# One product of a two-level Strassen scheme moved from a plain blocked product to an inner seven, with its operand sums kept in DRAM

## The chip, the cores and the metric

The kernel runs on one core of a Trainium2 chip. The time is the device time of one execution in microseconds (us); the kernel before has a median of 562.96 us over 3 runs (562.48 to 563.15). Lower is better. The engines are called as in the profile: PE (matrix products), DVE (vector), ACT (scalar), POOL (GpSimd), and SP, which here only issues DMAs. ACT and POOL issue DMAs too.

## The reference

Two layers on 16 graphs of 1024 nodes and 64 channels, with one 1024 x 1024 matrix `adj`:

```
# layer 0
Q, K, V = x Wq' + bq, x Wk' + bk, x Wv'
s = softmax(Q K', over the queries) ;  x = layernorm(x + (s adj) V)
# layer 1, both supports are adj
x1 = adj x ;  x2 = 2 adj x1 - x ;  x = layernorm(x + [x, x1, x2, x1, x2] weight + bias)
```

All is float32. Layer 1 can be written with two products by `adj`: with the five blocks W0..W4 of `weight`, z = x (W1 + W3) + adj (2 x (W2 + W4)), and the layer is x + x (W0 - W2 - W4) + bias + adj z. The change lies in the second product, adj z.

## The kernel before, in words

`xs` holds x with the nodes on the partitions (8 blocks of 128 nodes, index k) and 8 pairs of graphs (index p, 2 x 64 channels each). So adj z is a product of 1024 x 1024 by 1024 x 1024. It is done in Winograd's form of Strassen's scheme: seven products of 512 x 512 blocks, numbered 1 to 7. The left operand of product n is `SIDE[n]` (a block of adj or a sum of blocks, on chip), the right one is `B_F[n]` (a block of z or a sum). Most of these products are cut once more in the same way ("an inner seven"): class `Inner` (L931) forms four sums of quarters of the left operand (`of_a`), four of the right (`of_b`), and `Inner.step` (L953) runs one of seven 256 x 256 x 512-column pieces: four matmuls of 256 columns (`product`, L863) and then one to three additions of the result to its places (`step`, L872). The order is `STEPS`; `CHAIN = {6: 1, 3: 5, 4: 7}` says that the pieces 6, 3 and 4 add onto the PSUM bank of 1, 5 and 7. Such a piece can start only when the bank's earlier contents have been read out. `TO` says to which quarters a piece is added: 9 additions of 128x512 for seven pieces.

The work around the change, in program order (the order is written by hand; each engine runs its own instructions in that order, and an instruction that waits holds all behind it on its engine):

- Before adj z, the product for z itself is done. Its products 3 and 4 are inner sevens (`z3`, `z4`, L1104 to L1109). The sums of `SIDE[3]` for z3 are made by POOL into the two tiles `V` (`own(1)`), which product 5 of adj z overwrites later.
- adj z runs its products 1, 2, 5, 6 and 7 as inner sevens. While product 6 runs, POOL makes the left sums of product 7. Product 7 (L1177) is written to `W`, which takes the place of `SIDE[1]`. While product 7 runs, `added` (L987, its DMAs are L991 in the profile) issues six DMAs from POOL that add the tiles V and U to `xs` on their way (512 KB each, `accum_op=ADD`): V to rows k 4 to 7 and V to rows k 0 to 3 of the pairs 4 to 7, then U to rows k 4 to 7 of the pairs 0 to 3 (L1202).
- Then `wide_step` (L1185) does product 3 plainly: for each of four row blocks four matmuls of 512 columns over k, and one addition of 128x512 into `xs` (L1194). Product 4 follows in the same way, with its last row blocks cut narrower (L1220 to L1223).
- `add_w` (L1053) adds W to `xs` on DVE: twice to pairs 4 to 7, and twice (L1213, L1216) to pairs 0 to 3, rows k 4 to 7, which are the rows that product 4 writes.
- The last layernorm is done in pieces (`Norm`, L996) as rows come complete: `square` on ACT, `variance` (a DVE reduction, a DVE addition, and a power of -1/2 on POOL, L494), `out` (the scaling, and the DMA of the result). With `fast` the scaling of two row blocks is two DVE instructions, without it sixteen ACT instructions of 128x64 each. The four pieces of pairs 4 to 7 are `late[0]` to `late[3]` (rows 4-5, 6-7, 0-1, 2-3), the seven pieces of product 4 are `norms`.

Of the kernel before, what the change touches and what calls it, by code (L numbers as in the profile page):

```python
# [9 lines left out]
FP = mybir.dt.float32  # L10
AF = mybir.ActivationFunctionType
ALU = mybir.AluOpType
# [14 lines left out]
def gnn_kernel(  # L27
# [13 lines left out]
    nc = tc.nc  # L41
    N, B, C = out.shape
    P = 128
    K8 = N // P
    NP = B // 2
    HP = NP // 2
    H = 512
# [14 lines left out]
    dram = ctx.enter_context(tc.tile_pool(name="dram", bufs=2, space=bass.MemoryType.DRAM))  # L62
# [21 lines left out]
    xs = big.tile([P, NP, K8, P], FP, tag="xs", name="xs")  # L84
# [86 lines left out]
    K4 = K8 // 2  # L171
    Q = H // 2
    S = big.tile([P, 3, K4, H], FP, tag="s", name="S")

    def a_block(r, c):

        return aT[:, K4 * c : K4 * (c + 1), H * r : H * (r + 1)]

    SIDE = {
        1: a_block(0, 0), 2: a_block(0, 1), 3: S[:, 2], 4: a_block(1, 1),  # L180
        5: S[:, 0], 6: S[:, 1], 7: a_block(1, 0),
    }
# [12 lines left out]
    def quarter(big_tile, h, r, c):  # L195

        t = big_tile[:, K4 * r : K4 * (r + 1), h * H + c * Q : h * H + (c + 1) * Q]
        return t.rearrange("p k (q f) -> p q k f", q=2)
# [361 lines left out]
    t = [quarter(XB, 0, r, c) for r, c in ((0, 1), (0, 0), (1, 0), (1, 1))]  # L560
    hop_0 = Hop(lambda r, c: x_quarter(0, r, c), into(UY, 0), t, u, FIRST)
    t = [quarter(XB, 1, r, c) for r in range(2) for c in range(2)]
# [156 lines left out]
    def whole_run():  # L719
        hop, n, group = runs.pop(0)  # L720
        po = f_tile(f"p{n}")
        hop.product(po, n, group, True)
        return lambda: hop.evict(po, n, group)

    late = [whole_run() for _ in range(2)]
    tail, before = None, None
    for p in range(NP):
        q = p - 1
        for m in range(K8):
# [17 lines left out]
            late = []  # L747
# [105 lines left out]
    q = NP - 1  # L853
    for_pool, for_vector = [], []

    def behind(pool=2, vector=1):

        for _ in range(min(vector, len(for_vector))):
            for_vector.pop(0)()
        for _ in range(min(pool, len(for_pool))):  # L860
            for_pool.pop(0)()
# [24 lines left out]
    t = [quarter(UY, 0, r, c) for r in range(2) for c in range(2)]  # L886
# [13 lines left out]
    def z_block(r, c):  # L900
        return XB[:, K4 * r : K4 * (r + 1), ts(c, H)]

    T_F = [UY[:, K4 * r : K4 * (r + 1), ts(c, H)] for r in range(2) for c in range(2)]
    B_F = {
        1: z_block(0, 0), 2: z_block(1, 0), 3: z_block(1, 1),
        5: T_F[0], 6: T_F[1], 7: T_F[2], 4: T_F[3],
    }
# [10 lines left out]
    def tiles(*tags):  # L918
        return [
            att.tile([P, N], FP, tag=tag, name=f"in_{tag}", bufs={"e": 4, "xT": 2, "GT": 2}.get(tag, 1))  # L920
            for tag in tags
        ]

    def blocks_of(t, n):

        return [
            t_[:, ts(j, 2 * n)].rearrange("p (k f) -> p k f", k=2)
            for t_ in t for j in range(N // (2 * n))
        ]
# [28 lines left out]
    def of_full(n, tags):  # L958

        t = tiles(*tags)  # L960
        return Inner(
            n, lambda r, c: B_F[n][:, 2 * r : 2 * r + 2, ts(c, Q)],
            blocks_of(t[:2], Q), blocks_of(t[2:], Q),
        )

    def of_z(n, sa, tb):

        return Inner(n, lambda r, c: hop_z.side[n][:, c, 2 * r : 2 * r + 2], sa, tb)
# [7 lines left out]
    def own(c):  # L976

        t = [att.tile([P, 2, K4, P], FP, tag="e", name=f"own{c}", bufs=4) for c in range(2)]
        return t, lambda r, c: t[c][:, :, 2 * r : 2 * r + 2].rearrange("p q g f -> p g q f")

    def in_x(r, c):
        def d(r_, c_):
            p, k = HP * c + 2 * c_, K4 * r + 2 * r_
            return xs[:, p : p + 2, k : k + 2].rearrange("p q g f -> p g q f")
        return d

    def added(t, r, c):  # L987

        def do(j):
            p = HP * c + 2 * j  # L990
            nc.gpsimd.dma_start(xs[:, p : p + 2, K4 * r : K4 * (r + 1)], t[j], accum_op=ALU.add)  # L991
        return [lambda j=j: do(j) for j in range(2)]
# [55 lines left out]
    W = SIDE[1].rearrange("p k (q f) -> p k q f", f=P)  # L1048
# [4 lines left out]
    def add_w(c, i):  # L1053

        x_ = xs[:, HP * c : HP * (c + 1), K4 + i : K4 + i + 2]
        w_ = W[:, i : i + 2].rearrange("p k q f -> p q k f")
        nc.vector.tensor_tensor(x_, w_, x_, ALU.add)
# [33 lines left out]
    U, d_u = own(0)  # L1091
# [5 lines left out]
    for kk, banks in (0, None), (2, (w[1], w[0])):  # L1097
# [4 lines left out]
    V, d_v = own(1)  # L1102
    t = [v.rearrange("p q k f -> p (q k f)") for v in V]
    z3 = of_z(  # L1104
        3, blocks_of(t, Q),
        [SIDE[1][:, k, 0:Q].rearrange("p (k f) -> p k f", k=2) for k in range(K4)],
    )
    t = tiles(*X[:3])
    z4 = of_z(4, blocks_of(t[:2], Q), blocks_of(t[2:], P))  # L1109
    for do in added(U, 0, 0) + z3.sums(z3.of_a) + z4.sums(z4.of_a):  # L1110
        do()
    z_step(1, 1)
    for evict in both(mix, q, K8 - 4):
# [19 lines left out]
    def next_banks(n):  # L1133
        b = turn[:n]
        turn[:] = turn[n:] + b
        return b

    for z_n, d in (z3, in_z(0, 1)), (z4, in_z(1, 0)):
        b4 = next_banks(4)
# [7 lines left out]
    b4 = next_banks(4)  # L1147
# [10 lines left out]
    b4 = next_banks(4)  # L1158
# [4 lines left out]
        if i in (0, 2, 4):  # L1163
            (norm.square, norm.variance, norm.out)[i // 2]()
    seven = of_full(7, X)
    for_pool += seven.sums(seven.of_a)
    for_vector += sums_z[2] + seven.sums(seven.of_b, nc.vector)
    b4 = next_banks(4)
    for n in STEPS:
# [5 lines left out]
    b4 = next_banks(4)  # L1175
    norm = Norm(2, 2, 0, HP, False)
    for i, n in enumerate(STEPS):  # L1177
        seven.step(n, b4, d_w, True)
        if i == 1:
            for_pool += added(V, 1, 1) + added(V, 0, 1)  # L1180
        behind(4)
        if i in (0, 2, 4):
            (norm.square, norm.variance, norm.out)[i // 2]()

    def wide_step(n, r, c, i, cols):  # L1185

        po = next_banks(1)[0][:, 0 : cols.stop - cols.start]
        for k in range(K4):
            nc.tensor.matmul(  # L1189
                po, SIDE[n][:, k, ts(i, P)], B_F[n][:, k, cols], start=k == 0, stop=k == K4 - 1  # L1190
            )
        p = HP * c + cols.start // P
        x_ = xs[:, p : p + (cols.stop - cols.start) // P, K4 * r + i]
        nc.vector.tensor_tensor(x_, po.rearrange("p (q f) -> p q f", f=P), x_, ALU.add)  # L1194
        return K4 * r + i, p, (cols.stop - cols.start) // P

    add_w(1, 0)
    late = [Norm(k, 2, HP, HP, fast) for k, fast in ((4, False), (6, False), (0, True), (2, True))]
    late[0].square()
    add_w(1, 2)  # L1200
    late[1].square()
    for do in added(U, 1, 0):  # L1202
        do()
    for i in range(K4):
        wide_step(3, 0, 1, i, slice(0, H))
        if i < 3:
            late[i].variance()
        if i == 1:
            late[2].square()
        elif i == 2:  # L1210
            late[0].out()
            add_w(0, 0)
        elif i == 3:  # L1213
            late[3].square()
            add_w(0, 2)
            late[3].variance()  # L1216
            late[1].out()

    norms = []
    for step_, (i, cols) in enumerate((  # L1220
        (0, slice(0, H)), (1, slice(0, H)), (2, slice(0, Q)), (2, slice(Q, H)),
        (3, slice(0, Q)), (3, slice(Q, Q + P)), (3, slice(Q + P, H)),
    )):  # L1223
        k, p, n = wide_step(4, 1, 0, i, cols)
        norms.append(Norm(k, 1, p, n))
        if i < 3:
            norms[-1].square()
            (late[2], late[3], *norms)[step_].out()
            norms[-1].variance()
        else:  # L1230
            if i == 3 and step_ == 4:
                count[0] = 0
            norms[-1].small_variance()
            if step_ == 4:
                norms[2].out()
# [42 lines left out]
```

## Time and profile before

| | us |
|---|---|
| median of 3 runs | 562.96 |
| the profiled execution, its own time | 563.39 |
| its span in the profile | 561.6 |
| PE busy | 551.7 (98%) |
| DVE busy | 436.5 (78%) |
| ACT busy | 264.4 (47%) |
| POOL busy | 113.3 (20%) |
| product 3 of adj z on PE | 527.34 to 541.07 |
| product 4 of adj z on PE | 541.07 to 555.06 |

The span is what the profile covers; the time of an execution is a little longer. The lines of product 3 and 4 are instructions on L1189. The profile counts a float32 matmul as two. "Idle before" an instruction is followed by what ended the idling; a DMA row of POOL is the time in which POOL writes the transfer's descriptors, not the transfer.

### The profile page before, as it was taken

How to read it: one execution, taken by the hardware profiler on the slowest of the kernel's cores; microseconds unless marked ns; L12 is line 12 of the kernel's file. 1: busy time of each engine (PE TensorE's matmuls, PEld its weight loads, DVE VectorE, ACT ScalarE, POOL GpSimd, SP SyncE). 2: the span in 40 equal slices, each digit the busy share in tenths (PEclk: the TensorE clock that was granted, in tenths of full speed). 3: DMA queues.
4: the chain of work that ended last, by engine and by line, in shares of the span. 5: the costliest groups of instructions: out<-in, count | busy, mean ns of one | idle time of the engine just before them, and what ended most of it. 6: DMA issues, size and time to landing. Idle time of an engine off the chain costs nothing.

```text
span 561.6 us, 14524 instructions
## 1 busy us (share of the span) xinstructions
PE 551.7 (98%) x6150; PEld 407.2 (73%) x6150; DVE 436.5 (78%) x730; ACT 264.4 (47%) x595; POOL 113.3 (20%) x75
## 2 busy tenths in 40 slices
PE   8999999999999999999999999999999999999995
PEld 6767657567776777777777787777678789888644
DVE  0789888878789888788888888888737575789787
ACT  1133446546646655755765566675522300032571
POOL 0000000200200100020020001002002795594685
PEclk9999999999999999999999999999999999999999
DMA  7902002022002102102201210200201400001955
GB/s 239 365 12 76 2 1 78 2 76 77 3 39 81 35 2 101 53 1 78 77 1 40 76 40 2 76 2 2 78 1 65 86 1 1 1 1 37 181 139 169
DMA packets 26371, 33.67 MB, mean 60 GB/s; under 512 B 3010, under 2 KB 19650, under 8 KB 25922
## 3 DMA queue, kind: packets, MB, share of 16 engines
q1 hardware_dynamic: 23714, 28.35, 15.1%
q0 software_dynamic: 2176, 4.19, 4.2%
q8 instruction: 48, 0.79, 0.6%
q10 hardware_dynamic: 416, 0.20, 0.1%
q14 instruction: 17, 0.14, 0.1%
HBM read 16.48 MB, written 12.06 MB: 51 GB/s over the span
## 4 chain that ended last, share of the span: by engine, by line
PE 80%; issue 7%; DVE 6%; DMA 2%; ACT 2%; POOL 1%; SPq 1%; POOLq 0%; ACTq 0%; DVEq 0%
PE p L267 19%; PE sc L410 17%; PE acc L447 14%; PE w L867 13%; PE small L528 3%; PE w L1189 3%; PE small L472 2%; PE pu L257 2%; PE wide L867 2%; DVE nm L417 2%; POOL rstd L494 1%; PE pv L257 1%; PE small L367 1%; DMA aT<-in_adjT_dram 1%; ACT e L426 1%
## 5 line engine op out<-in xcount | busy, mean ns | idle before, releaser
L410 PE MATMUL sc<-xT,GT 64*64 64x512 f32 x1024 | 240.6, 591 | 0.2 <-ACT e L426 0.2
L447 PE MATMUL acc<-e,us 64*64 64x512 f32 x1008 | 238.6, 590 | 0.0
L426 ACT ACTIVATE e<-sc,nm 128x1024 f32<-128x1024 f32 x128 | 142.5, 1113 | 108.9 <-DVE nm L417 100.0
L417 DVE TENSOR_REDUCE nm<-sc 128x1 f32<-128x1024 f32 x128 | 155.5, 1215 | 3.4 <-PE sc L410 2.9
L494 POOL TENSOR_TENSOR rstd<-var,expo 128x16 f32<-128x16 f32 (+3 forms) x21 | 50.0, 2383 | 408.8 <-DVE var L492 408.5
L447 PEld LDWEIGHTS acc<-e,us 64*64 64x64 f32 x1008 | 70.4, 133 | 24.0 <-issue 7.5
L410 PEld LDWEIGHTS sc<-xT,GT 64*64 64x64 f32 x1024 | 69.3, 132 | 11.2 <-issue 5.4
L267 PE MATMUL p<-UY,aT 64*64 64x256 f32 x480 | 59.1, 376 | 0.0
L267 PE MATMUL p<-XB,S 64*64 64x256 f32 x480 | 58.0, 377 | 0.0
L267 PE MATMUL p<-UY,S 64*64 64x256 f32 x384 | 44.8, 376 | 0.0
L267 PE MATMUL p<-XB,aT 64*64 64x256 f32 x352 | 43.1, 377 | 0.0
L267 PEld LDWEIGHTS p<-XB,S 64*64 64x64 f32 x480 | 32.6, 133 | 13.6 <-issue 3.2
L267 PEld LDWEIGHTS p<-UY,aT 64*64 64x64 f32 x480 | 33.6, 133 | 11.6 <-issue 1.2
L528 PE MATMUL small<-w,x0T_k 64*64 64x192 f32 x384 | 39.5, 323 | 0.0
L528 PEld LDWEIGHTS small<-w,x0T_k 64*64 64x64 f32 x384 | 26.6, 133 | 11.9 <-issue 5.0
L267 PEld LDWEIGHTS p<-UY,S 64*64 64x64 f32 x384 | 27.8, 133 | 7.1 <-issue 0.4
L267 PE MATMUL p<-xs,aT 64*64 64x256 f32 x256 | 31.2, 377 | 0.0
L267 PE MATMUL p<-xs,S 64*64 64x256 f32 x256 | 31.1, 377 | 0.0
L267 PEld LDWEIGHTS p<-XB,aT 64*64 64x64 f32 x352 | 24.9, 133 | 8.3 <-issue 1.3
L880 ACT COPY own<-w 128x512 f32<-128x512 f32 x8 | 4.5, 588 | 54.6 <-PE w L867 54.6
L538 ACT ACTIVATE UY<-small 128x128 f32<-128x128 f32 x48 | 13.3, 276 | 28.2 <-PE small L528 28.2
L426 ACT ACTIVATION_READ_ACCUMULATOR e<-sc,nm 128x1 f32 x128 | 24.8, 194 | 0.0
(211 smaller groups left out, 898.7 us busy)
## 6 DMA issues: line engine op xcount, KB each, us to landing
d<-blocks SPq DMA_DIRECT2D x15, 512.0 KB, 2.6
x0T<-d SPq DMA_DIRECT2D x32, 128.0 KB, 2.9
xs<-own POOLq DMA_DIRECT2D x8, 512.0 KB, 7.5
xT<-d SPq DMA_DIRECT2D x28, 128.0 KB, 2.8
out_dram<-xs SPq DMA_DIRECT2D x14, 256.0 KB, 2.2
xs<-in_x_dram SPq DMA_DIRECT2D x3, 1024.0 KB, 8.0
aT<-in_adjT_dram SPq DMA_DIRECT2D x8, 256.0 KB, 6.0
aT<-in_adjT_dram SPq DMA_DIRECT2D x4, 512.0 KB, 7.6
```

Of the source, the lines that this page charges most:

```text
L257: nc.tensor.matmul(po[t * w : (t + 1) * w], SIDE[n][:, k, j : j + w], self.side[n][:, :, k, :], start=start, stop=True, skip_group_check=True,
L267: nc.tensor.matmul(po[half[c]], SIDE[n][half[t], k, i * P + c * C : i * P + (c + 1) * C], self.side[n][half[t], :, k, :], start=t == 0 and ...
L410: nc.tensor.matmul(sc[half[c], ts(h, H)], GT[p][half[j], c * H + m * C : c * H + (m + 1) * C], xT(p)[half[j], ts(h, H)], start=True, stop= ...
L417: nc.vector.tensor_reduce(nm, sc, AX.X, ALU.max, negate=True)
L426: nc.scalar.activation(e, sc, AF.Exp, bias=nm, accum_out=sm[:, j : j + 1])
L447: nc.tensor.matmul(ACC[p, h][half[j]], us[half[t], j], es[j][half[t], ts(h, H)], start=m == 0 and t == 0, stop=m == K8 - 1, skip_group_che ...
L472: nc.tensor.matmul(o[half[t], ts(k, C)], OT[p][half[j], n : n + C], wv2[half[j], half[j]], start=True, stop=True,)
L494: nc.gpsimd.tensor_tensor(rstd, var, expo[:, 0:n], ALU.pow)
L528: nc.tensor.matmul(t[half[c], 0:3, k], X0T[p][half[j], n : n + C], w3[half[j]], start=True, stop=True,)
L538: nc.scalar.activation(part(UY, j), t[:, 0], AF.Copy)
L867: nc.tensor.matmul(po[:, ts(g, b.shape[1] * P)], a[:, k, ts(g, P)], b[:, :, k, :], start=start and g == 0 and k == 0, stop=True, skip_grou ...
L1189: nc.tensor.matmul(po, SIDE[n][:, k, ts(i, P)], B_F[n][:, k, cols], start=k == 0, stop=k == K4 - 1)
```

## The change

Product 3 becomes an inner seven. Its left sums are those that z3 made from the same `SIDE[3]`: after they are made, SP writes both V tiles to a DRAM tile `kept`, and reads them back into the tiles `o` and `t` after the first piece of product 7 is issued, when product 6 has done with those tiles. Its right sums are four POOL additions of 128x512 into `SIDE[5]`, put in POOL's list behind the left sums of product 7. The pieces run in the order 1, 2, 5, 6, 3, 7, 4. The two DVE additions of W to pairs 0 to 3 become four DMAs from POOL, 256 KB each, that add one row block of W each (runs of 512 bytes in `xs`); they stand in POOL's order right behind the six adding DMAs and ahead of all powers of `late`. `late[2]` is scaled by ACT in place of DVE, and some parts of `late` stand at other places between the pieces.

```diff
-    for do in added(U, 0, 0) + z3.sums(z3.of_a) + z4.sums(z4.of_a):
+    for do in added(U, 0, 0) + z3.sums(z3.of_a):
+        do()
+
+    kept = dram.tile([P, 2, N], FP, tag="kept", name="kept", bufs=1)
+    V3 = [v.rearrange("p q k f -> p (q k f)") for v in V]
+    for j in range(2):
+        nc.sync.dma_start(kept[:, j], V3[j])
+    for do in z4.sums(z4.of_a):
         do()
...
     seven = of_full(7, X)
-    for_pool += seven.sums(seven.of_a)
+    blocks = [SIDE[5][:, k].rearrange("p (k f) -> p k f", k=2) for k in range(K4)]
+    for_pool += seven.sums(seven.of_a) + [
+        lambda x=x: nc.gpsimd.tensor_tensor(*x)
+        for x in Inner(3, lambda r, c: B_F[3][:, 2 * r : 2 * r + 2, ts(c, Q)], blocks, blocks).of_b
+    ]
...
     for i, n in enumerate(STEPS):
         seven.step(n, b4, d_w, True)
+        if i == 0:
+            back = tiles("o", "t")
+            for j in range(2):
+                nc.sync.dma_start(back[j], kept[:, j])
+            three = Inner(
+                3, lambda r, c: B_F[3][:, 2 * r : 2 * r + 2, ts(c, Q)], blocks_of(back, Q), blocks
+            )
...
-    late = [Norm(k, 2, HP, HP, fast) for k, fast in ((4, False), (6, False), (0, True), (2, True))]
+    late = [Norm(k, 2, HP, HP, fast) for k, fast in ((4, False), (6, False), (0, False), (2, True))]
     late[0].square()
     add_w(1, 2)
     late[1].square()
     for do in added(U, 1, 0):
         do()
-    for i in range(K4):
-        wide_step(3, 0, 1, i, slice(0, H))
-        if i < 3:
-            late[i].variance()
-        if i == 1:
-            late[2].square()
-        elif i == 2:
-            late[0].out()
-            add_w(0, 0)
-        elif i == 3:
-            late[3].square()
-            add_w(0, 2)
-            late[3].variance()
-            late[1].out()
+    for k in range(K4):
+        nc.gpsimd.dma_start(xs[:, 0:HP, K4 + k], W[:, k, 0:HP], accum_op=ALU.add)
+    b4 = next_banks(4)
+    then = {
+        0: late[0].variance, 2: late[1].variance, 3: late[0].out, 4: late[2].square,
+        5: late[1].out, 6: late[3].square,
+    }
+    for i, n in enumerate((1, 2, 5, 6, 3, 7, 4)):
+        three.step(n, b4, in_x(0, 1))
+        if i in then:
+            then[i]()
+    late[2].variance()
...
         k, p, n = wide_step(4, 1, 0, i, cols)
         norms.append(Norm(k, 1, p, n))
+        if step_ == 0:
+            late[3].variance()
```

## The prediction

> **What bounds the kernel now.** I read the page first: PE is busy for 98% of the span, and 80% of the chain that ended last is PE.
>
> ```profile
> PE 551.7 (98%) x6150; PEld 407.2 (73%) x6150; DVE 436.5 (78%) x730; ACT 264.4 (47%) x595; POOL 113.3 (20%) x75
> PE 80%; issue 7%; DVE 6%; DMA 2%; ACT 2%; POOL 1%; SPq 1%; POOLq 0%; ACTq 0%; DVEq 0%
> ```
>
> That is a mean over the kernel. The change works in the last 50 us, so I read PE's timeline there: products 3 and 4 are two rows of L1189, without a gap.
>
> ```profile
> 525.61 1.89 PE L867 MATMUL w<-UY,in_xT 128*128 128x256 f32 x8
> 527.34 13.90 PE L1189 MATMUL w<-XB,S 128*128 128x512 f32 x32
> 541.07 13.99 PE L1189 MATMUL w<-UY,aT 128*128 128x512 f32 x56
> ```
>
> Then the other engines' timelines in the same stretch, POOL's first:
>
> ```profile
> 508.87 2.25 POOL L951 TENSOR_TENSOR in_xT<-aT,in_xT 128x512 f32<-128x512 f32 x1
> 518.50 1.24 POOL L991 DMA_DIRECT2D xs<-own  x1 [7.38 <-DVE own L1173]
> 521.10 3.67 POOL L991 DMA_DIRECT2D xs<-own  x3 [1.36 <-DVE own L1173]
> 523.37 4.40 POOL L494 TENSOR_TENSOR rstd<-var,expo 128x16 f32<-128x16 f32 x1
> 526.25 3.96 POOL L991 DMA_DIRECT2D xs<-own  x2
> 535.16 8.66 POOL L494 TENSOR_TENSOR rstd<-var,expo 128x16 f32<-128x16 f32 x3 [4.95 <-DVE var L492]
> ```
>
> A power takes 2.9 us for 16 numbers per partition (8.66 / 3). The rows overlap, but as a sum they fit a serial engine: from 521.10 to 530.21 there are five DMA issues and a power, 5 x 1.24 + 2.90 = 9.1. POOL's free time is 7.38 us before the first issue and 4.95 us before the first power of `late`. In ACT's and DVE's timelines I read who waits on this:
>
> ```profile
> 533.05 0.69 DVE L1194 TENSOR_TENSOR xs<-w,xs 128x512 f32<-128x512 f32 x1 [2.43 <-DMA xs<-own]
> 538.12 3.93 ACT L1042 ACTIVATE xs<-xs,rstd 128x64 f32<-128x64 f32 x16 [1.32 <-POOL rstd L494]
> 549.00 0.63 ACT L1007 ACTIVATE aT<-xs 128x512 f32<-128x512 f32 x1 [1.55 <-DVE xs L1194]
> ```
>
> ACT scales `late[0]` the moment its power is done (538.06). DVE's first addition of product 3 waits for the adding DMAs. How long those run, the table of short stretches shows (its last three columns: granted clock, share of the DMA engines, GB/s):
>
> ```profile
> 519.00:520.00 1.00, 1.00 (x6) 0.87 (x5) 1.00 (x2) 0.00 (x0) 0.74 (x1) 1.00 0.00 0
> 520.00:521.00 1.00, 1.00 (x6) 0.90 (x5) 1.00 (x2) 0.37 (x1) 0.00 (x0) 1.00 0.80 145
> 537.00:538.00 1.00, 1.00 (x3) 0.38 (x2) 0.16 (x1) 0.00 (x0) 1.00 (x1) 1.00 1.09 301
> 538.50:539.00 0.50, 0.50 (x3) 0.26 (x2) 0.50 (x2) 0.50 (x3) 0.50 (x1) 1.00 0.13 39
> ```
>
> The six additions (3.15 MB) keep the DMA engines full from 520.2 to 538.6. Their descriptors are all written by 530.2, but the last, the two U tiles, land at about 538.6, 11.8 us after the later issue (the longest landing in POOL's rows).
>
> **The change, part by part.**
>
> *Product 3 on PE.* 16 matmuls of 512 columns take 13.73 us (527.34 to 541.07), 0.858 each; a piece of four matmuls of 256 columns takes 1.73 (525.61 to 527.34), seven 12.11. That is -1.62 us if PE waits for nothing. It will wait: the fourth piece (6) adds onto the bank of piece 1, which DVE empties only once the V tiles have landed (533.05 to 533.65), where PE would be there at 532.5: 1.1 late. The fifth (3) needs the bank of piece 5, behind a reduction of 1.21, its addition of 0.17 and two evictions of 0.6 on DVE: 536.3 against 535.4. The last (4) needs that of piece 7, DVE having to do five evictions and the next reduction in between: about 540.8. Product 3 ends on PE near 542.5, 1.4 later than now: the gain is gone by this alone.
>
> *DVE.* Nine evictions of 0.6 for four, +3.0; without two additions of W (1.22 each) and the scaling of `late[2]` (1.28), -3.7. Near nothing.
>
> *ACT.* +16 instructions, 3.93 us (the row at 538.12), between the squares of the first two pieces of product 4.
>
> *POOL's four sums for the right side.* 1.27 to 2.25 each by the L951 rows (1.74, 1.27, 2.13, 2.25 just before). They start at 511.1 in the gap of 7.38 us: 5.1 to 9.0, I take 7.2, so the gap is just filled. If it is not, the first adding DMA goes up to 1.6 later. DVE's additions of two on-chip operands were longer while POOL worked (L916 2.08 and 1.69 against 1.22), so the sums of V and U (L1173), on which the issues wait, may come 0 to 2.3 later. I take 1.0 for both together: the U tiles land at 539.6, between 538.6 and 541.5.
>
> *Kept in DRAM.* Two stores of 512 KB behind POOL's last sum at 447; SP's next order is at 505.7, so nothing is held. Two loads: tile o is free at 511.8, t at 515.25 (PE's rows of product 6); 512 KB land in 2.6 (d<-blocks) to 7.6 us (the loads of adj), so by 518 to 523, while PE wants them at 530.8. At the long end they share the DMA engines with the first additions for 2.6 us, which is inside the 541.5 above. SP's next result waits for ACT until 529.8. Cost nothing.
>
> *The four DMAs that add W.* They add to the rows of `xs` to which the U DMAs add, and the first waits for these. The wait stands on POOL's queue, and behind it stand all powers of `late` and `norms`. So POOL stops from about 531 to 539.6, writes four sets of descriptors, and only then does the first power. No row shows an adding DMA of 512-byte runs: the eight that exist have 256 runs of 2 KB and take 1.24 us to issue, these have 512 runs; by count 1.24 to 2.48 each, four of them 5.0 to 9.9. I take 1.6 each, nearer the row because a part of it should be per DMA: 6.4. Their transfer, 1 MB, is 5.5 us by bytes (at 190 GB/s) and 22 us if a packet of 512 B costs like one of 2 KB (16 engines, 2048 packets, 0.172 us each). Even then the last lands near 565, before the eviction that needs it (568 below). So only the issue is on the path.
>
> *Sum.* 539.6 + 6.4 + 2.9: the first power of `late` ends at 548.9 (T), where it ended at 538.06. From T the order on ACT is: scale `late[0]` 3.93, square `late[2]` 1.02, scale `late[1]` 3.93, square `late[3]` 1.02, square of product 4's first row block 0.60, scale `late[2]` 3.93, square of the second 0.60: T + 15.0. The second, third and fourth power (each 2.9, the inputs of the third and fourth ready at T + 6.5 and T + 11.3) don't outlast it. From the end of that second square (549.63 above) the run before needed 561.6 - 549.63 = 12.0 us to its end, by DVE's and POOL's alternation over the narrow blocks, which is unchanged. So the end is T + 27.0 = 575.9; the execution's own time is 1.79 above the span (563.39 - 561.6), and the median 0.43 below that execution: 577.3 us. PE's later end (542.5 + 14 = 556.5) is well inside.
>
> The Trainium skill bears on this in "DMA: Bandwidth & Descriptors", section "Anatomy of one DMA — SWDGE (gpsimd) path": DMA engines don't wait on semaphores, any wait happens on the issuing sequencer before dispatch. This speaks against the change, and POOL's 7.38 us before its first issue is such a wait. The same section puts one DMA of this kind at 2.0 us + bytes / 436 GB/s, 3.2 us for 512 KB; the trace has 5.0 to 11.8, since the additions run at about 190 GB/s behind each other. By the page the U tiles would land at 533.4 and the estimated sum would be 571.1; the trace's landing decides.
>
> **The rivals.**
>
> *POOL is not held* (the W additions go out without waiting, or their issue hides). For it: four issues of 1.24 fit POOL's idle 4.95 us. Against: same rows of `xs`, transfers in flight until 538.6. Then T stays 538.06, and ACT's added scaling still makes the end T + 27.0 = 565.1: 566.4 us, slower too.
>
> *Faster: PE is the bound and the shorter product comes through.* For it: 98% busy, no gap in product 3. Then 562.96 - 1.62 = 561.3 us. It decides if T + 27.0 falls below 561.6, so if the first power ends before 534.6; its input exists only at 535.1 today, since DVE waits for V until 533.05. It would need the additions to land some 4 us earlier, and nothing makes them.
>
> *The transfers of W become the last wait.* If a packet of 512 B cost half as much again as one of 2 KB, the last would land at 541 + 33 + 2 = 576, 7.9 us of work follow (568.0 to 575.9 in my sum): 585 us. Against: they carry a quarter of the bytes.
>
> **How the numbers follow.** A change under 0.2% (1.1 us) can't be told from none. POOL held, 0.86; not held, 0.07; W's transfers last, 0.03; faster, 0.02; something that cancels to within 0.2%, 0.02. The forecast is 577.3. Its bounds: landing 538.6 and issue 1.24 give T = 546.5 and 574.9; landing 541.5 and issue 2.48 give T = 554.3 and 582.7. The stretch of 27 us is put together from rows of other neighbours, 1 us either way: 573.5 to 584. Slower 0.96, within 0.2% 0.02, faster 0.02.
>
> **What would show it.** POOL's timeline: idle for 7 to 9 us up to about 539 to 541, ended by a DMA on `xs`, then four issues on the new line; the first power of 128x16 after that ends at 546 to 554. ACT: the scaling of `late[0]` waits for POOL more than 8 us. DVE: idle for several us ahead of the third reduction of `late`, as ACT's square comes late. PE: gaps of about 1 us ahead of the fourth, fifth and last piece, product 3 ending near 542.5; the loads of `kept` landing before 523. Wrong it would be if the power ran beside the waiting DMAs, if POOL's four sums outlast their gap by several us, or if the additions land at another time than now.

## The result and the profile after

| | before | after |
|---|---|---|
| median, us | 563.01 | 576.23 (575.72 to 577.24) |
| profiled execution, us | 563.39 | 576.89 |
| its span, us | 561.6 | 575.1 |
| PE busy | 551.7 (98%) | 551.9 (96%) |
| POOL busy | 113.3 | 124.6 |

The ratio of the times is 1.0239, 95% interval 1.0228 to 1.025: 13.2 us slower, forecast 577.3. PE is as busy in microseconds as before. Its last product ends at 556.71, 18.4 us ahead of the span's end; before it was 6.5 us (555.06 of 561.6).

POOL's timeline after (start, duration, engine, line, operation, count; in brackets the idle time before and what ended it):

```profile
519.21 1.24 POOL L991 DMA_DIRECT2D xs<-own  x1 [2.58 <-DVE own L1184]
526.09 3.96 POOL L991 DMA_DIRECT2D xs<-own  x2
540.20 5.21 POOL L1223 DMA_DIRECT2D xs<-aT  x4 [10.15 <-DVE xs L882]
543.24 8.01 POOL L494 TENSOR_TENSOR rstd<-var,expo 128x16 f32<-128x16 f32 x2
554.88 2.90 POOL L494 TENSOR_TENSOR rstd<-var,expo 128x16 f32<-128x16 f32 x1 [3.64 <-DVE var L492]
```

POOL's new sums (L1175, from 510.18 to 516.62) fit their gap of 7.38 us, of which 2.58 are left. The last U issue ends at 530.05, and then POOL idles for 10.15 us. The row names DVE as what ended it; the instruction waits for several things, and the chain of waits (rows under 0.1 us are left out) has the one that counts:

```profile
526.85 12.78 DMA xs<-own
539.71 0.49 issue
540.20 5.21 POOL xs L1223 x4
545.41 2.96 POOL rstd L494
```

That is the forecast's path: the U tiles land at 539.64, four issues, then the first power of `late`, which ends at 548.37 in place of 538.06. ACT and DVE wait behind it, ACT for its first scaling and DVE for ACT's square:

```profile
548.40 3.93 ACT L1042 ACTIVATE xs<-xs,rstd 128x64 f32<-128x64 f32 x16 [14.95 <-POOL rstd L494]
```

```profile
553.38 1.22 DVE L488 TENSOR_REDUCE var<-aT 128x16 f32<-128x1024 f32 x1 [10.87 <-ACT aT L1007]
```

Further on the same chain leaves ACT: after the square of `late[3]` come its reduction on DVE, the fourth power on POOL and its scaling on DVE.

```profile
558.14 1.23 DVE var L488
559.65 2.91 POOL rstd L494
562.58 1.29 DVE xs L1036 x2
```

PE, with product 3 as pieces of L867 from 526.42 and product 4 on L1207:

```profile
526.42 3.62 PE L867 MATMUL w<-XB,S 128*128 128x256 f32 x16
529.87 1.89 PE L867 MATMUL w<-S,in_o 128*128 128x256 f32 x8
532.05 1.97 PE L867 MATMUL w<-S,in_o 128*128 128x256 f32 x8 [0.28 <-DVE xs L882]
535.22 1.99 PE L867 MATMUL w<-XB,in_t 128*128 128x256 f32 x8 [1.20 <-DVE xs L882]
537.05 1.89 PE L867 MATMUL w<-S,in_t 128*128 128x256 f32 x8
539.81 1.96 PE L867 MATMUL w<-S 128*128 128x256 f32 x8 [0.88 <-DVE xs L882]
541.61 13.10 PE L1207 MATMUL w<-UY,aT 128*128 128x512 f32 x48
```

Product 3 takes 541.61 - 526.42 = 15.2 us, against 13.7 before: 12.1 of work and about 3 of waiting ahead of the three chained pieces. Each of them waits for an eviction on DVE (the addition that reads a PSUM bank out).

### The profile page after: what moved, and what is told of

The parts are those of the page before. It is cut to its first block, busy times and chain, and to the rows that moved or that the text cites. A ratio compares the mean times of both kernels' runs of the same rounds, so it can differ in the third digit from the quotient of the medians.

```text
span 575.1 us, 14621 instructions
## 1 busy us (share of the span) xinstructions
PE 551.9 (96%) x6174; PEld 412.9 (72%) x6174; DVE 437.6 (76%) x731; ACT 267.9 (47%) x611; POOL 124.6 (22%) x83
## 4 chain that ended last, share of the span: by engine, by line
PE 73%; issue 8%; DVE 8%; POOL 4%; DMA 3%; ACT 3%; SPq 0%; POOLq 0%; DVEq 0%; ACTq 0%
PE p L267 18%; PE sc L410 17%; PE acc L447 14%; PE w L867 9%; PE small L528 3%; POOL rstd L494 3%; PE pu L257 3%; DMA xs<-own 2%; PE small L472 2%; PE wide L867 2%; DVE nm L417 2%; PE pv L257 1%; PE small L367 1%; DVE var L488 1%; ACT xs L1042 1%
## 5 line engine op out<-in xcount | busy, mean ns | idle before, releaser
L494 POOL TENSOR_TENSOR rstd<-var,expo 128x16 f32<-128x16 f32 (+3 forms) x21 | 52.1, 2590 | 406.5 <-DVE var L492 406.2
L1042 ACT ACTIVATE xs<-xs,rstd 128x64 f32<-128x64 f32 x80 | 19.6, 333 | 21.1 <-POOL rstd L494 21.1
```

What stands on the lines that cost most here:

```text
L494: nc.gpsimd.tensor_tensor(rstd, var, expo[:, 0:n], ALU.pow)
L1042: nc.scalar.mul(row, row, rstd[:, j : j + 1])
```

## Experiments

Theory A: the time is lost because POOL's queue stands still until the U tiles land and then writes four sets of descriptors, with every power of the last layernorm behind it. Rivals: B, the 16 scalings added to ACT; C, PE's waits inside the inner seven; D, the transfers of W themselves. All ratios are to the kernel before on the same chip. The chip differs from run to run, so two runs are compared by how far each is above the kernel before on its own chip: the change is 13.2 us above it.

### W added by DVE again

```diff
-    for k in range(K4):
-        nc.gpsimd.dma_start(xs[:, 0:HP, K4 + k], W[:, k, 0:HP], accum_op=ALU.add)
...
         if i in then:
             then[i]()
+        if i in (5, 6):
+            add_w(0, 2 * (i - 5))
```

> The change without its four adding DMAs of W: the two DVE additions of W are back, behind the sixth and the seventh piece of product 3. Theory A (POOL's queue held by the wait for the U tiles and by four issues): the first power of late ends near 537 to 538 in place of 548.4, the order on ACT is as in the change, so the end is 27 us later, about 565: 565.5 us, some 10.7 of the 13.2 us are gone and some 2.5 stay. Rival B (ACT's 16 added scalings are the cost): it stays at 575 or more. Rival C (PE's waits inside the inner seven are the cost): 575 as well, since PE's order is unchanged.

Measured: 566.48 us, ratio 1.0059 (1.0044 to 1.0074), 3.6 us above the kernel before. POOL's timeline:

```profile
526.92 3.96 POOL L991 DMA_DIRECT2D xs<-own  x2
534.89 5.80 POOL L494 TENSOR_TENSOR rstd<-var,expo 128x16 f32<-128x16 f32 x2 [4.01 <-DVE var L492]
```

The first power ends at 537.8, and the span at 564.6, 26.8 later, as in the change (26.7). 9.6 of the 13.2 us are gone; 3.6 stay, 1.1 more than expected. ACT's added scalings and the order on PE are as in the change, so B and C can't be the large part. Whether it is the queue or the transfers, the next run tells.

### The four DMAs moved behind two powers

```diff
-    for k in range(K4):
-        nc.gpsimd.dma_start(xs[:, 0:HP, K4 + k], W[:, k, 0:HP], accum_op=ALU.add)
...
+        if i == 2:
+            for k in range(K4):
+                nc.gpsimd.dma_start(xs[:, 0:HP, K4 + k], W[:, k, 0:HP], accum_op=ALU.add)
```

> The change with its four W DMAs only moved: they are issued behind the first two powers of late in POOL's order, everything else kept (ACT scales late[2]). Theory A (it is what stands behind the wait on POOL's queue that costs, not the additions by DMA): first power at 537 to 538, issues from 540.7 to 546, W's first row block landed by 547 to 548: 566.5 us, like the kernel with W on DVE (566.5), up to 567.5. Rival (the transfers of W or their sharing of the DMA engines): 572 or more.

Measured: 565.77 us, ratio 1.0059 (1.0044 to 1.0074), 3.3 us above the kernel before. POOL's timeline:

```profile
534.94 5.80 POOL L494 TENSOR_TENSOR rstd<-var,expo 128x16 f32<-128x16 f32 x2 [4.02 <-DVE var L492]
540.70 5.24 POOL L1233 DMA_DIRECT2D xs<-aT  x4
```

The same four DMAs, the same bytes, and 9.9 of the 13.2 us are gone: only their place in the queue is different. The DMAs even go out at nearly the same time as in the change (540.70 and 540.20), so D is out. The row shows no idle time before them: when POOL has done two powers, they wait for nothing.

### Eight DMAs in place of four

```diff
     for k in range(K4):
-        nc.gpsimd.dma_start(xs[:, 0:HP, K4 + k], W[:, k, 0:HP], accum_op=ALU.add)
+        for q in (0, 2):
+            nc.gpsimd.dma_start(xs[:, q : q + 2, K4 + k], W[:, k, q : q + 2], accum_op=ALU.add)
```

> The change with its W additions issued as eight DMAs of two pairs each (128 KB) in place of four of 256 KB: the same bytes in the same runs of 512 B. Theory A, with the issue paid per DMA (1.3 us each): 5.2 us more ahead of the first power, which ends near 553.6: 581.4 us. If the issue is paid per run of 512 B: 576.2. If the transfer of W sets the end (rival): 576 too, since the bytes are the same.

Measured: 579.86 us, ratio 1.0311 (1.0295 to 1.0326), 17.4 us above the kernel before and so 4.2 more than the change, where 5.2 were expected.

```profile
536.21 1.20 POOL L1224 DMA_DIRECT2D xs<-aT  x1 [6.34 <-DMA xs<-own]
539.36 8.60 POOL L1224 DMA_DIRECT2D xs<-aT  x7 [1.95 <-DMA xs<-own]
```

An issue costs 1.20 to 1.30 us whether it has 256 runs (1.24 for the V and U tiles, 1.23 here) or 512 (1.30 in the change), so nearly all of it is paid by the DMA, not by the run. The expectation missed that a DMA of two pairs needs one U tile only: the first one went out at 536.2, when the first tile had landed, and one issue was hidden. That a wait for data, not DVE, ends POOL's idling is plain in these rows.

### W by DMA in the kernel before

The DMAs alone, with product 3 plain and `late[2]` scaled by DVE:

```diff
+    for k in range(K4):
+        nc.gpsimd.dma_start(xs[:, 0:HP, K4 + k], W[:, k, 0:HP], accum_op=ALU.add)
     for i in range(K4):
         wide_step(3, 0, 1, i, slice(0, H))
...
-            add_w(0, 0)
...
-            add_w(0, 2)
```

> The kernel before with one part of the change alone: the four adding DMAs of W in place of the two DVE additions, at the change's place in POOL's order; product 3 stays plain. Theory A: POOL waits until the U tiles land (538.6), issues for 5.2 and then does the first power: it ends near 547 where it ended at 538.1; the rest of the order is that of before, 23.5 us to the end: 570.5 of span, about 572 us, 9 us slower than before. Rivals B and C (the inner seven or ACT's scaling are the cost): 563 us.

Measured: 572.38 us, ratio 1.0167 (1.0152 to 1.0182).

```profile
539.10 5.21 POOL L1205 DMA_DIRECT2D xs<-aT  x4 [9.13 <-DMA xs<-own]
542.14 10.87 POOL L494 TENSOR_TENSOR rstd<-var,expo 128x16 f32<-128x16 f32 x3
```

ACT begins the first scaling at 547.31 and the span ends at 570.6, 23.3 later (before: 23.5). The DMAs alone cost 9.5 us; with the first two runs this settles A, by adding the cause and by taking it away.

### `late[2]` scaled by DVE again

```diff
-    late = [Norm(k, 2, HP, HP, fast) for k, fast in ((4, False), (6, False), (0, False), (2, True))]
+    late = [Norm(k, 2, HP, HP, fast) for k, fast in ((4, False), (6, False), (0, True), (2, True))]
```

> The change with one part undone: late[2] is scaled by DVE again, two instructions of 0.64 in place of sixteen on ACT (3.93). Theory A: the first power still ends at 548.4, and from there the path to the end runs over the square of late[3], its power and its scaling on DVE, which the 3.93 us on ACT don't delay: 576.2, at most 0.7 either way. Rival B (ACT's added scalings are the cost): 572.3 or less.

Measured: 577.0 us, ratio 1.0251 (1.0236 to 1.0266). That is 0.8 us above the expectation, just outside its 0.7; 3.93 us fewer on ACT gain nothing, so B falls. In its ACT timeline the square of product 4's second row block, which in the change came right after these scalings, now waits for DVE instead. It starts 13.8 us behind the start of ACT's first scaling (548.10), in the change 13.9 (562.28, 548.40):

```profile
561.92 0.63 ACT L1007 ACTIVATE aT<-xs 128x512 f32<-128x512 f32 x1 [3.66 <-DVE xs L1212]
```

### Less work on PE, in the kernel before

This kernel leaves out a quarter of product 3, the matmuls with k = 3, so its output lacks that part; it serves only to time a shorter product.

```diff
-        for k in range(K4):
+        last = K4 - (n == 3)
+        for k in range(last):
             nc.tensor.matmul(
-                po, SIDE[n][:, k, ts(i, P)], B_F[n][:, k, cols], start=k == 0, stop=k == K4 - 1
+                po, SIDE[n][:, k, ts(i, P)], B_F[n][:, k, cols], start=k == 0, stop=k == last - 1
             )
```

> The kernel before with plain product 3 on 12 of its 16 matmuls (k = 3 is left out, so that rows 0 to 511 of the pairs 4 to 7 lack a quarter of product 3): PE has 3.4 us less in the place where the change saves 1.6. If PE bounds the end: 559.4 us. If the chain of the last layernorm does (first power waiting for the tiles V, then ACT's scalings, then DVE): 562.8, within 0.4.

Measured: 563.12 us, ratio 1.0007 (0.9998 to 1.0017). Product 3 and 4 on PE:

```profile
527.58 10.46 PE L1190 MATMUL w<-XB,S 128*128 128x512 f32 x24
537.88 13.99 PE L1190 MATMUL w<-UY,aT 128*128 128x512 f32 x56
```

Product 4 starts 3.2 us earlier and the span is 561.7. PE, busy for 98% of the span, does not set the end here: 3.4 us less work in the place where the change saves 1.6 gains nothing, so a seven that ran without a wait would have gained nothing in the order of before either. The chain of waits of the kernel before runs through product 3 and 4 on PE until 544.54; here it runs from the V tiles over DVE, POOL's first power and ACT, and from 522.80 on PE is not in it. So the two legs were about equally long. The first power starts at 535.40 (before 535.16), since its input waits for the V tiles:

```profile
533.28 0.69 DVE L1195 TENSOR_TENSOR xs<-w,xs 128x512 f32<-128x512 f32 x1 [2.42 <-DMA xs<-own]
```

### The inner seven alone, and three other orders of it

With W added by DVE (as in the first diff) and `late[2]` scaled by DVE (as above), what is left of the change is the seven itself:

```diff
-    for k in range(K4):
-        nc.gpsimd.dma_start(xs[:, 0:HP, K4 + k], W[:, k, 0:HP], accum_op=ALU.add)
...
-    late = [Norm(k, 2, HP, HP, fast) for k, fast in ((4, False), (6, False), (0, False), (2, True))]
+    late = [Norm(k, 2, HP, HP, fast) for k, fast in ((4, False), (6, False), (0, True), (2, True))]
...
+        if i in (5, 6):
+            add_w(0, 2 * (i - 5))
```

> The inner seven of product 3 with its operands kept in DRAM and its sums on POOL, but W added by DVE and late[2] scaled by DVE, as before. Theory A: the powers are free, first one ending near 537 to 538; late[2] and late[3] come complete later than before, since the seven's pieces finish their quarters at the end of the product (the squares stand behind the scalings on ACT): fourth power at 14 us behind the first, end near 564.5, 565 us. If the shorter product of 12.1 in place of 13.7 us on PE were worth what it says: 561.4 us.

Measured: 566.16 us, ratio 1.0061 (1.0044 to 1.0078): 3.3 us slower, with the powers free (the first starts at 534.09). Before, the square of `late[2]` starts when two row blocks of product 3 are complete. The seven completes these rows with its fifth piece, and the square stands on ACT behind the scaling of `late[0]`. The square in the kernel before, and in this one:

```profile
535.75 1.06 ACT L1007 ACTIVATE aT<-xs 128x1024 f32<-128x1024 f32 x1 [2.13 <-DVE xs L1194]
```

```profile
540.89 1.04 ACT L1007 ACTIVATE aT<-xs 128x1024 f32<-128x1024 f32 x1
```

So I turned the order of the squares, on top of that kernel:

```diff
-        0: late[0].variance, 2: late[1].variance, 3: late[0].out, 4: late[2].square,
-        5: late[1].out, 6: late[3].square,
+        0: late[0].variance, 2: late[1].variance, 4: late[2].square, 5: late[0].out,
+        6: late[3].square,
...
-        if i in (5, 6):
-            add_w(0, 2 * (i - 5))
-    late[2].variance()
+        if i == 5:
+            add_w(0, 0)
+            late[2].variance()
+    add_w(0, 2)
+    late[1].out()
```

> The inner seven alone (W by DVE, late[2] scaled by DVE), with the order on ACT turned: the squares of late[2] and late[3] ahead of the scalings of late[0] and late[1], and the reduction of late[2] ahead of the last piece's addition on DVE. Theory (the seven finishes its quarters late and the squares stand behind 3.93 us scalings on ACT): third power ends near 544 and fourth near 549.5 in place of 548 and 551.2; 565.3 us against 566.2. The rest of the loss against before, about 2.4 us, stays, since late[2] can't be squared before the fifth piece, 539, against 535.8 before.

Measured: 565.19 us, ratio 1.0049 (1.0034 to 1.0064), 2.7 us above the kernel before on its chip, where the seven alone was 3.3 above it: 0.6 us back, expected 0.9. ACT's timeline:

```profile
539.62 1.06 ACT L1007 ACTIVATE aT<-xs 128x1024 f32<-128x1024 f32 x1 [5.51 <-DVE xs L882]
549.17 0.62 ACT L1007 ACTIVATE aT<-xs 128x512 f32<-128x512 f32 x1
```

The square of `late[2]` still waits for DVE until 539.62. That of product 4's first row block stands at 549.17, where it stood at 546.83 before: 2.3 us, about the loss that is left (2.7). Next I moved the reductions on DVE behind the evictions that PE's chained pieces wait for:

```diff
-        0: late[0].variance, 2: late[1].variance, 4: late[2].square, 5: late[0].out,
-        6: late[3].square,
+        2: late[0].variance, 4: late[2].square, 5: late[0].out, 6: late[3].square,
...
-        if i == 5:
-            add_w(0, 0)
-            late[2].variance()
+        if i in (4, 5):
+            late[i - 3].variance()
...
+    add_w(0, 0)
     add_w(0, 2)
     late[1].out()
```

> As the run with the squares first (inner seven, W by DVE, late[2] scaled by DVE), and the reductions of late[0] and late[1] on DVE moved behind the evictions that PE's chained pieces wait for (behind the third and the fifth piece's), the two W additions behind the last piece's. Theory (the rest of the inner seven's loss is PE waiting for banks that DVE empties behind those reductions, so that late[2] is squared only at 539.6): product 3 ends on PE near 540.2 in place of 542.3, the square of late[2] starts near 537.5, that of product 4's first row block near 547 as before the change: 563.2 us, equal to before within 0.2%. If the loss has another cause: 565.

Measured: 566.17 us, ratio 1.0057 (1.0043 to 1.0071), not the 563.2 expected. The five times lie between 564.35 and 566.58, and the profiled one is the fastest of them: its span is 562.6, product 3 ends on PE at 540.98 (expected near 540.2) and the first row block's square starts at 546.75, as expected. The wait of the chained pieces has mostly moved: PE loses nothing before the fifth piece now, but 2.02 us before the last, in the seven alone 0.88. In this trace the first power waits for the reduction, the reduction for an eviction, and that eviction for the second V tile:

```profile
532.69 0.69 DVE L882 TENSOR_TENSOR xs<-w,xs 128x512 f32<-128x512 f32 x1 [1.53 <-DMA xs<-own]
533.30 1.21 DVE L488 TENSOR_REDUCE var<-aT 128x16 f32<-128x1024 f32 x1
```

So this order hangs the chain on when that tile lands. Why the other four executions are slower stays open, since they have no trace. The profile of the next run, in the same order, has DVE's wait end at 533.98, 1.29 later; but 0.89 of that is there when product 3 begins (527.20 against 526.31), so only 0.4 can be the tile's. With the scalings of `late[1]` and `late[3]` cut into parts on ACT (by `parts`, shown in the last experiment):

```diff
-    late[1].out()
+    on_act = late[1].parts()
+    for _ in range(4):
+        on_act.pop(0)()
...
-            (late[2], late[3], *norms)[step_].out()
+            if step_ == 0:
+                late[2].out()
+                on_act += late[3].parts()
+            elif step_ > 1:
+                norms[step_ - 2].out()
+            for _ in range((10, 8, 3, len(on_act))[step_]):
+                on_act.pop(0)()
```

> The same, and the scalings of late[1] and late[3] cut into parts on ACT behind the squares of product 4 (late[3] no longer on DVE): the square of the first row block near 545, DVE's chain 1.3 us shorter, PE's end 0.9 earlier than before: 562.0 us, 0.998 of before. If the parts delay the squares as in the run with parts on ACT alone: 563.

Measured: 564.34 us, ratio 1.0031 (1.0018 to 1.0044), where 562.0 or, if the parts delay the squares, 563 was expected. The best order of the seven that I found, and still behind the kernel before.

### Scalings moved from DVE to ACT in the kernel before

If DVE's chain set the end alone, taking work off it should beat the kernel before:

```diff
+        def parts(self):
+            todo = []
...
+                for j in range(2 * n):
+                    row = rows_[:, j // 2, j % 2]
+                    todo.append(lambda row=row, r=rstd[:, j : j + 1]: nc.scalar.mul(row, row, r))
...
-            (late[2], late[3], *norms)[step_].out()
+            if step_ == 0:
+                late[2].out()
+                on_act = late[3].parts()
+            elif step_ == 2:
+                on_act += norms[0].parts()
+            elif step_ == 3:
+                norms[1].out()
+            for _ in range((5, 6, 3, len(on_act))[step_]):
+                on_act.pop(0)()
```

> The kernel before, nothing of the change; only the scalings of late[3] and of product 4's first row block go from DVE (1.28 + 0.61 us) to ACT, cut into parts of 5, 6, 3 and 10 instructions of 0.25 us behind the squares of product 4, where ACT idles. Theory (the end is set by DVE's chain in product 4, not by PE): DVE's chain is 1.9 us shorter, of which PE's end at 555.1 leaves some 0.9 to 1.0: 562.0 us, 0.998 of before. If DVE does not bind, or ACT's parts delay the squares: 563 or more.

Measured: 562.71 us, ratio 0.9999 (0.999 to 1.0008): the gain expected, to 562.0, does not come. DVE's timeline:

```profile
550.12 0.69 DVE L488 TENSOR_REDUCE var<-aT 128x8 f32<-128x512 f32 x1 [0.70 <-ACT aT L1007]
551.82 0.42 DVE L488 TENSOR_REDUCE var<-aT 128x4 f32<-128x256 f32 x1 [0.48 <-ACT aT L1007]
```

Where the scaling stood, DVE now waits for the square of the row block that it has just evicted. In the kernel before, a scaling (548.88 to 550.08) filled that wait: the reduction behind it starts at 550.08 there and at 550.12 here. So this stretch is a chain that goes to and fro between DVE and ACT, and the scaling beside it was mostly cover.

## Why the prediction was right

*The path.* The steps up to the first power are in the chain of waits as forecast: U tiles landing (539.6 forecast, 539.64 measured), the issues, the power. It ended at 548.4, forecast 548.9, and from there the end took 26.7 us, forecast 27.0. That last stretch was right in size but not in every step. I had said that the later powers don't outlast ACT's order. ACT's second square ends at 562.89 (14.5 behind the first power, forecast 15.0), but DVE's next reduction starts only at 563.79, since the fourth power ends at 562.56 and the scaling of `late[3]` behind it has to be done first. ACT being half a microsecond faster made up for this.

*The issues* were the one term without a row: taken as 1.6 each between 1.24 and 2.48, they are 1.30 (5.21 for four). The nearer end was right and my part for more runs was not there; some 0.5 us pass between the landing and the first issue, which I had not counted and which made up for half of it.

*Product 3 on PE.* The forecast said that the gain is eaten, 15.2 us in place of 13.7; that is what it took. The split was off: before the fourth piece PE lost 0.45 (forecast 1.1), before the fifth 1.44 (0.9), before the last 1.03. The first addition of the plain product waits until 533.05, that of the seven, which writes two of the four pairs and so needs one V tile only, until 531.21. None of it is on the path of the change. By the run with less PE work a shorter product 3 is worth nothing in the order of before; what the longer one costs there, no run isolates.

*POOL's four sums* took 6.4 us (forecast 7.2) in a gap of 7.38. DVE's additions of on-chip operands beside them took 1.16 and 1.31 us, against 0.67 without POOL's sums, and so the first adding DMA came later. That the U tiles landed within 0.1 of the forecast, 1.0 later than before, is partly luck. The trace of the change runs 0.84 us ahead of that of before already at an adding DMA of POOL (437.23 against 438.07), in front of anything that was changed, and 0.92 ahead at the start of product 3. Counted from that start, the first adding DMA is 1.6 later (-7.21 against -8.84), and the tiles land 13.2 us behind it in the change (12.6 with `late[2]` on DVE, 12.5 with eight DMAs), against 11.4 in the kernel before with W by DMA: 1.1 to 1.8 later, inside the range but above the 1.0 that I took.

*The copy in DRAM* cost nothing: the loads went out at 511.1 and 514.5 and landed within 3.2 us, PE wanted them from 529.9.

*W's transfers.* The DMA engines are busy with them from 542 to 548, on average at 174 GB/s: by bytes, the lower of my bounds. The 190 GB/s that I took for the V and U tiles was too high for the additions alone, since 0.52 MB of results move in the same stretch; the six tiles, 3.15 MB in 18.4 us, are 171. The rival that they come last never stood near. The Trainium skill's figure for a DMA issued by POOL, in "DMA: Bandwidth & Descriptors", "Anatomy of one DMA — SWDGE (gpsimd) path" (2.0 us + bytes / 436 GB/s; the section doesn't say that it holds for adding DMAs), gives an estimate of 2.6 us for 256 KB; the median from issue to landing here is 5.0, with four behind each other. Its other sentence there, that the wait is on the issuing sequencer and not in the DMA engine, is what the run with the moved DMAs shows: 9.9 us for their place in the queue.

*The rival "POOL is not held"* had 566.4 us as its price; the two runs that free the queue measured 566.48 and 565.77. It was right that the change is slower even then, and ACT's order behind the first power (T + 27 against 23.5) was its cause: in the runs 26.8 and 26.9. That the added scaling on ACT is what makes it longer was not: taken away (the inner seven alone), the end is still 27.1 us behind the first power, since the square of `late[3]` stands as late. The path has two legs of about equal length there, the one over the scaling of `late[2]` on ACT and the one over the fourth power, and I had named the first only.

## What to carry to other kernels

A DMA that must wait for an earlier one is issued from an engine's queue, and everything behind it on that engine waits too (here POOL stood for 10.15 us): look up what stands there before a copy or addition is "moved to DMA", and put it behind work that is due earlier. A busy share of 98% doesn't say that an engine sets the end: read what the last rows wait for, and test it by taking work away. A scheme with fewer multiplications that completes all its results at the end delays whoever works on the first results (here 3.3 us for the seven alone).

## What was not expected of the hardware

The issue of an adding DMA cost 1.20 to 1.31 us, nearly independent of its 256 or 512 runs and of 128, 256 or 512 KB. Runs of 512 B were added at 174 GB/s, no slower than runs of 2 KB (171 by their bytes alone, with results moving beside them).
